# Second attention of a two-attention block: the sync queue's order written out by hand, raw weights requested and converted at set turns

## The chip, the cores and the metric

The kernel runs on one core of one Trainium2 chip. The metric is the time of one execution in microseconds (us) of device time. Before the change it is 1457.29 us, the median of three runs (1456.06 to 1458.13). The engines are TensorE (PE, matrix products), VectorE (DVE), ScalarE (ACT), GpSimd (POOL) and SyncE (SP); SP computes nothing and issues nearly all DMA transfers, in the order of its own queue.

## The reference

The input is x, 1024 tokens of 512 numbers. Four stages follow each other, each with a layernorm ahead of it and a residual sum behind it:

```python
x = x + attn_a(layernorm(x))   # 32 heads of 16, 8 groups of keys and values
x = x + ffn(layernorm(x))      # base matrix plus 2 of 8 low-rank experts per token
x = x + attn_b(layernorm(x))   # 32 query heads of 128, 8 key/value groups, 4-bit weights, causal
x = x + ffn(layernorm(x))      # the same ffn again
```

The change lies in the third, the second attention:

```python
def _dequant_matmul(x, qw, scales):
    w = (qw.astype(float32) - 8.0) * repeat(scales, 128, axis=0)
    return x @ w
q, k, v = dequant matmuls of x;  q, k = rope(q), rope(k)
scores = causal(q @ k.T / sqrt(128));  attn = softmax(scores);  ctx = attn @ v
return _dequant_matmul(ctx, qw_o, scales_o)
```

The weights qw_q, qw_k, qw_v and qw_o arrive as int32 numbers from 0 to 15.

## The kernel before, in words

The first attention, the first ffn, the second attention and the second ffn run one after another and overlap at their seams. The second attention occupies about 545 to 1390 us of the profiled execution.

**Heads and turns.** The loop over 32 query heads n (group g = n // 4, place in the group j = n % 4) has eight turns per head. Each turn takes one tile t of 128 query rows, in the order TURNS = 0, 6, 1, 7, 2, 4, 3, 5. In a turn PE makes the score product of the tile (L869); DVE adds the causal mask and finds the largest value (L877); ACT exponentiates (L881); DVE inverts the sum (L885); ACT divides (L886). One turn later `placed` has DVE transpose the tile in 32 by 32 blocks (L900), and when both tiles of a pair are done (pair 0: tiles 0 and 1, pair 1: 2 and 3, pair 2: 4 and 5, pair 3: 6 and 7) it issues four transfers on SP (L911) that put the blocks in place: 48 KB each for pair 0, 112 KB for pair 1, 176 KB for pair 2, 240 KB for pair 3. Pair 0 goes out after turn 3's score product, pair 3 after turn 4's, pair 1 after turn 7's, pair 2 after the next head's turn 0. The context products (L949) read them: `context(n, 0)` pairs 0 and 3, `context(n, 1)` pairs 1 and 2, three turns or more later.

**Two lanes of other work.** Between the turns PE is filled from two lists of generators, a `short` and a `long` one, by nominal costs and a share per turn. `short` holds the projections: in head n the queries of head n+1, in some heads the keys or values of the next group, and the output projection of the head before. A projection (`scaled`, L798 to L812) makes, for each half of the tokens, four pairs of products; ACT takes the first pair with its scale into an accumulator tile `acc` (L810), DVE adds the other three (L812). There are two `acc` tiles. For queries and keys `rotated` then needs the rotary embedding: two transfers on SP put the halves of `acc` crosswise into a tile `turned` (L822, L823; a "turned pair" below, of 128 KB each), and POOL computes `acc` times cosine (L824), `turned` times sine (L825) and their sum (L826). The output projection's fourth part goes through ACT (L987) and POOL (L988).

**Raw weights.** `whole_numbers` (L703) requests 256 KB of int32 weights on SP (L705) into a tile `r`, one buffer for each of the kinds q, k (keys and values share it) and o, and has POOL subtract 8 into a tile `w` (L706), two buffers for each kind. A new request waits until POOL has converted the tile in `r` before it; a conversion waits until PE is done with the `w` of two before it.

**Who sets the order.** Everything in the second attention is written under `manual_schedule(engines={PE})`: PE's queue keeps the order of the source. The other four queues are ordered by the scheduler of the language's tile layer, by its own estimate of when things are ready, so a request can stand in SP's queue well ahead of its place in the source or behind it. In the program that results, SP's queue before the change has, in a typical head, pair 0, the request for qwo, pair 3, turned pairs, a request for k or v, pair 1, pair 2, a turned pair, the request for q.

Of the kernel before, what the change touches and what calls it, by code (L numbers as in the profile page):

```python
# [12 lines left out]
F32R = mybir.dt.float32r  # L13
BF16 = mybir.dt.bfloat16
I32 = mybir.dt.int32
# [5 lines left out]
P = 128  # L21
S = 1024
C = 512
NC_ = C // P
NT = S // P
# [4 lines left out]
G = 8  # L30
# [11 lines left out]
def kernel(  # L42
# [630 lines left out]
    def attention_b():  # L673
# [5 lines left out]
        with ExitStack() as ph:  # L679
# [17 lines left out]
            def bank():  # L697
                return ac_ps.tile([P, C], F32, tag="acc", name="bank")

            def whole_numbers(kind, rows, n, bufs=2):  # L700

                r = work.tile([P, n], I32, tag=f"r{kind}", name="r", bufs=1)
                w = work.tile([P, n], F32R, tag=f"w{kind}", name="w", bufs=bufs)  # L703
                dst = r if len(rows.shape) == 2 else r.rearrange("p (c o) -> p c o", o=rows.shape[2])
                nc.sync.dma_start(dst, rows)  # L705
                nc.gpsimd.tensor_scalar_add(w, r, -ZERO)  # L706
                return w

            def input_weights(kind, qw, n):
                rows = qw[:, ts(n, DB)].rearrange("(c p) o -> p c o", p=P)  # L710
                return whole_numbers(kind, rows, NC_ * DB).rearrange("p (c o) -> p c o", o=DB)

            wks = {0: input_weights("k", qwk, 0)}
            wqs = {0: input_weights("q", qwq, 0)}
            wvs = {0: input_weights("k", qwv, 0)}
            wos = {0: whole_numbers("o", qwo[0:P, :], C)}
            nc.sync.dma_start(cos_sb, cos_t)

            nc.sync.dma_start(sin_sb[0:64], sin_t[64:128])
# [74 lines left out]
            def left(lane):  # L794
                return sum(item[1] for item in lane)
# [65 lines left out]
            def probabilities(n, t):  # L861

                qT, kT = qTs[n], kTs[n // J]
                keys = (t + 1) * P
                wide = t >= NT // 2 or (n == 0 and t == 1)
                sc = sc_ps.tile([P, S if wide else C], F32, tag=f"sc{wide}", name="sc")
                for k0 in range(0, keys, C):
                    k1 = min(k0 + C, keys)
                    nc.tensor.matmul(sc[:, k0:k1], qT[:, ts(t, P)], kT[:, k0:k1], start=True, stop=True)  # L869
# [12 lines left out]
                return p, total  # L882
# [7 lines left out]
            def placed(n, t, p):  # L890

                pair, first = t // 2, t // 2 * 2 + 1
                if t % 2 == 0 and pair > 1:
                    blocks[pair] = late[0].tile(
                        [P, J, (2 * first + 1) * 32], F32, tag=f"blocks{pair}", name="blocks", bufs=1
                    )
                at = t % 2 * first * 32
                nc.vector.transpose(  # L900
                    blocks[pair][:, :, at : at + (t + 1) * 32].rearrange("p j (k c) -> p k j c", c=32),
                    p.rearrange("p (k j c) -> p k j c", j=4, c=32),
                )
                if t % 2:
                    which = int(pair in SETS[1])
                    while any(m == n - 1 and int(u // 2 in SETS[1]) == which for m, u in lagging):
                        behind()
                    complete(("c", n - 1, which))
                    width = (2 * first + 1) * 32
                    for i in range(4):  # L910
                        nc.sync.dma_start(  # L911
                            place[pair][:, i],
                            blocks[pair][ts(i, 32), :, :width],
                        )
# [88 lines left out]
            with tc.manual_schedule(engines={mybir.EngineType.PE}):  # L1003
# [83 lines left out]
                    nc.vector.tensor_copy(flat[:, part.start : part.start + 1], total)  # L1087
                    nc.sync.dma_start(room[:, part], w_kept[:, part])

                def request(n):  # L1090

                    g, j = n // J, n % J
                    if j == 0 and 0 < g < G - 1:
                        wks[g + 1] = input_weights("k", qwk, g + 1)
                    if j == 2 and g + 1 < G:
                        wvs[g + 1] = input_weights("k", qwv, g + 1)

                for n in range(HEADS):
                    g, j = n // J, n % J
                    if j == 0 and 0 < g < G - 1:  # L1100
                        short.append([("k", g + 1), 16 * FAST, keys(g + 1)])
                    if j == 2 and g + 1 < G:
                        short.append([("v", g + 1), 16 * FAST, values(g + 1)])
                    if n + 1 < HEADS:
                        wqs[n + 1] = input_weights("q", qwq, n + 1)
                        short.insert(0, [("q", n + 1), 16 * FAST, queries(n + 1)])
                    shares = [
                        (left(lane) + LAST_LATER[i]) // NT
                        if n == HEADS - 1
                        else (left(lane) + LATER[i] - KEPT[i] - HELD[i] * (j % 2 == 0)) // NT  # L1110
                        if n
                        else left(lane) // 5
                        for i, lane in enumerate((short, long))
                    ]
                    for i, t in enumerate(TURNS if n else [0, 1, 2, 4, 3, 5, 6, 7]):
                        if n and i == 2:
                            wos[n] = whole_numbers("o", qwo[ts(n, P), :], C)
                        if i == 4:
                            request(n + 1)

                        p, total = probabilities(n, t)
                        lagging.append((n, t))
                        if fresh:
                            placed(*fresh.pop())
                        fresh.append((n, t, p))
                        if n == t == 0:
                            complete(("k", 0))
                            complete(("q", 0))
                            wks[1] = input_weights("k", qwk, 1)
                            short.append([("k", 1), 16 * FAST, keys(1)])  # L1130
                            shares[0] = left(short) // NT
                        fill(short, shares[0])
                        divided(p, total)
                        if n == HEADS - 1 and i:
                            reload(i - 1, total)
                        join()
                        if len(lagging) > LAG and lagging[0][0] < HEADS - 1:
                            behind()
                        fill(long, shares[1])
                    complete(("q", n + 1))  # L1140
                    if j == J - 1:
                        complete(("k", g + 1))


                xns = {
# [139 lines left out]
```

## Time and profile before

| | |
|---|---|
| median of three runs | 1457.29 us |
| profiled execution, first to last instruction (span) | 1454.8 us |
| what lies around the span, by the median | 2.5 us |
| mean granted TensorE clock | 0.994 |
| stretch 640 to 745 us (four heads): PE, DVE, ACT, POOL busy | 102.38, 93.88, 68.74, 64.15 us of 105 |
| one head in the middle of the loop | 24.9 to 27.8 us |

The profile is of one execution. A group line names the source line, the engine, what is written and read, the count, the busy time and the mean duration, and then the engine's idle time ahead of these instructions with what ended it. `SPq` is the SP queue: a line of its waits gives who waited for whom, total time, times, longest. In a timeline row the first number is the start, the second the duration (both us), and brackets hold idle time just before and what ended it; rows with x4 merge four instructions. PE's busy time is modelled and counts weight loading beside it separately (PEld).

### The profile page before, as it was taken

Reading aid. Unit: us, or ns where it says so; the run is one execution under the profiler, and the core shown is the slowest. Engines: PE = TensorE matmul, PEld = TensorE weight load, DVE = VectorE, ACT = ScalarE, POOL = GpSimd, SP = SyncE. Lnnn points to the kernel's source line nnn. Section 1 sums busy time; section 2 is a strip of 40 time slices with the busy share of each in tenths; the row PEclk is TensorE's granted clock in tenths of the full one; section 3 lists DMA queues with packets and bytes.
Section 4 is the critical chain, followed back from the end, with each engine's and each line's share of the span. In section 5 each row is a group of like instructions: output and inputs, shape, how many; then the busy total and the mean of one; then the engine's idle time right before and its main releaser. Section 6 shows DMA issues by size and latency. Waiting matters only on the chain.

```text
span 1454.8 us, 21185 instructions
## 1 busy us (share of the span) xinstructions
PE 1390.1 (96%) x6711; PEld 882.1 (61%) x6711; DVE 1190.2 (82%) x2491; ACT 868.6 (60%) x1642; POOL 539.7 (37%) x425
## 2 busy tenths in 40 slices
PE   6999999999999998999999999999999999999888
PEld 4444444444444545677777777776776777777664
DVE  4799979879892668798998988898898898989774
ACT  2176657657677226676676666666665676666630
POOL 4200000000000516556646646656566566544230
PEclk9999999999999999999999999999999999999999
DMA  4352423324240324655555655655556555555611
GB/s 126 59 103 46 72 36 62 54 39 73 40 133 2 99 73 110 144 142 149 131 143 143 145 134 135 150 141 135 148 133 150 140 137 134 136 136 120 182 65 58
DMA packets 136736, 158.48 MB, mean 109 GB/s; under 512 B 35008, under 2 KB 111488, under 8 KB 136496
## 3 DMA queue, kind: packets, MB, share of 16 engines
q1 hardware_dynamic: 136204, 156.49, 45.1%
q8 instruction: 54, 0.88, 0.3%
q0 software_dynamic: 352, 0.59, 0.2%
q14 instruction: 58, 0.48, 0.1%
q10 hardware_dynamic: 68, 0.03, 0.0%
HBM read 33.03 MB, written 6.05 MB: 27 GB/s over the span
## 4 chain that ended last, share of the span: by engine, by line
PE 70%; DVE 10%; DMA 9%; SPq 4%; POOL 3%; issue 2%; ACT 2%; ACTq 0%; POOLq 0%; DVEq 0%
PE pc L949 13%; PE sc L869 12%; PE po L408 7%; PE sc L334 7%; DVE m L343 6%; DMA xT<-blocks 6%; PE pp L799 4%; PE pp L798 4%; PE bank L607 4%; PE py L798 3%; SPq L911 3%; PE py L799 3%; DMA turned<-acc 3%; PE st L375 2%; PE py L448 2%
## 5 line engine op out<-in xcount | busy, mean ns | idle before, releaser
L387 ACT ACTIVATE pT<-st 128x512 f32<-128x512 f32 x512 | 264.6, 603 | 128.7 <-PE st L383 107.1
L343 DVE TENSOR_REDUCE m<-sc 128x1 f32<-128x512 f32 x512 | 319.8, 681 | 25.8 <-PE st L375 20.4
L869 PE MATMUL sc<-kT,qT 128*128 128x512 f32 (+3 forms) x768 | 291.6, 489 | 4.3 <-POOL qT L826 2.1
L881 ACT ACTIVATE x_sb<-x_sb,m 128x768 f32<-128x768 f32 (+7 forms) x256 | 196.9, 769 | 119.5 <-DVE m L877 116.8
L949 PE MATMUL pc<-xT,v_sb 128*128 128x256 f32 (+1 forms) x1024 | 242.0, 361 | 22.9 <-DMA xT<-blocks 22.0
L886 ACT ACTIVATE x_sb<-x_sb,total 128x768 f32<-128x768 f32 (+7 forms) x256 | 195.5, 772 | 70.7 <-DVE total L885 69.2
L949 PEld LDWEIGHTS pc<-xT,v_sb 128*128 128x128 f32 x1024 | 191.3, 190 | 59.5 <-issue 26.4
L877 DVE CUSTOM_DVE_ANT_0 x_sb<-sc,causal 128x768 f32<-128x768 f32 (+7 forms) x256 | 191.5, 748 | 36.4 <-PE sc L869 35.1
L334 PE MATMUL sc<-ks,qs 64*128 64x512 f32 x512 | 186.9, 448 | 5.3 <-DVE m L343 2.6
L798 PE MATMUL pp<-x_hl,w 128*128 128x512 f32 x384 | 183.9, 479 | 2.0 <-ACT acc L810 1.4
L869 PEld LDWEIGHTS sc<-kT,qT 128*128 128x128 f32 x768 | 138.3, 191 | 76.1 <-issue 61.2
L383 PE MATMUL st<-ms_q,ones 64*128 64x512 f32 x512 | 177.9, 413 | 0.7 <-DMA ms_q<-mT 0.7
L375 PE MATMUL st<-qs,ks 64*128 64x512 f32 x512 | 176.0, 423 | 1.4
L334 PEld LDWEIGHTS sc<-ks,qs 64*128 64x128 f32 x512 | 83.8, 184 | 146.1 <-DVE m L343 129.5
L799 PE MATMUL pp<-x_hl,w 128*128 128x512 f32 x384 | 153.4, 399 | 2.3 <-DVE x_hl L756 2.3
L900 DVE STREAM_TRANSPOSE blocks<-x_sb 128x640 f32<-128x640 f32 (+3 forms) x128 | 133.2, 1041 | 25.0 <-ACT x_sb L886 21.2
L812 DVE SCALAR_TENSOR_TENSOR acc<-pp,q_sc,acc 128x512 f32<-128x512 f32 x192 | 140.8, 733 | 14.1 <-ACT acc L810 10.3
L706 POOL TENSOR_SCALAR w<-r 128x512 fp32r<-128x512 int32 x80 | 119.6, 1495 | 80.3 <-PE pp L799 49.4
L824 POOL TENSOR_TENSOR qT<-acc,cos_sb 128x512 f32<-128x512 f32 x62 | 79.9, 1288 | 168.6 <-DVE acc L812 133.2
L127 POOL DMA_DIRECT2D shared<-in_b_base_dram x1 | 0.6, 563 | 367.3 <-DVE m L343 367.3
L408 PE MATMUL po<-pT,v_sb 128*32 128x512 f32 x1024 | 136.6, 604 | 0.0
L798 PE MATMUL py<-ctx,w 128*128 128x512 f32 x256 | 132.9, 519 | 2.1 <-ACT acc L810 1.4
(174 smaller groups left out, 2138.3 us busy)
## 6 DMA issues: line engine op xcount, KB each, us to landing
xT<-blocks SPq DMA_DIRECT2D x128, 240.0 KB, 4.4
xT<-blocks SPq DMA_DIRECT2D x128, 176.0 KB, 3.2
turned<-acc SPq DMA_DIRECT2D x160, 128.0 KB, 2.6
pT<-x_sb SPq DMA_DIRECT2D x128, 112.0 KB, 2.7
qs<-q_hl SPq DMA_DIRECT2D x128, 64.0 KB, 2.5
qs<-shared SPq DMA_DIRECT2D x128, 64.0 KB, 2.5
r<-in_qwq_dram SPq DMA_DIRECT2D x32, 256.0 KB, 2.8
r<-in_qwo_dram SPq DMA_DIRECT2D x32, 256.0 KB, 2.7
```

The lines of the kernel that those rows point to most:

```text
L334: nc.tensor.matmul(sc, qs[pair % NS][rows, jj, ts(t, P)], ks[pair // 2 % NS][rows, ts(half, C)], start=True, stop=True,)
L343: nc.vector.tensor_reduce(ms[pair][:, at : at + 1], sc, AX.X, ALU.max, negate=True)
L375: nc.tensor.matmul(st, ks[pair // 2 % NS][rows, ts(kt, P)], qs[pair % NS][rows, u // 2, ts(u % 2, C)], start=True, stop=False,)
L387: nc.scalar.activation(pTs[pair, kt][:, u], st, AF.Exp, scale=DA**-0.5)
L408: nc.tensor.matmul(po[ts(u, 32), :], v_sb[:, kt, pair // 2, :], pT[:, u], start=(kt == 0), stop=(kt == NT - 1),)
L798: nc.tensor.matmul(ps, lhsT, high, start=True, stop=False)
L799: nc.tensor.matmul(ps, lhsT, low, start=False, stop=True)
L869: nc.tensor.matmul(sc[:, k0:k1], qT[:, ts(t, P)], kT[:, k0:k1], start=True, stop=True)
L877: nc.vector.tensor_tensor_reduce(p, sc[:, :keys], causal[:, S - keys :], -1.0, BIG, ALU.add, ALU.min, m)
L881: nc.scalar.activation(p, p, AF.Exp, bias=m, scale=-1.0, accum_out=total)
L886: nc.scalar.activation(p, p, AF.Copy, scale=total)
L949: nc.tensor.matmul(pc[:, 2 * P * i + lo : 2 * P * (i + 1)], v_sb[:, k, ts(g, DB)], some, start=(k == 0), stop=(k == 2 * pair + 1),)
```

## The change

In the second attention alone, three things:

- `whole_numbers` is split into `request`, which issues the transfer into `r`, and `whole_numbers`, which converts it into `w`.
- The requests and conversions stand at set turns of a head. `ask(n, i)`, after the score product of turn i: at turn 1 the raw queries' weights of head n+2 (before, those of head n+1 at the head's start), at turn 2 those of a key or value projection that head n+1 begins, at turn 3 the output weights of head n. `convert(n, i)`, ahead of the score product: at turns 5, 6 and 7 the same three.
- The loop over the heads stands under a second `manual_schedule` for SP, so that SP's queue too keeps the order of the source within it. POOL, DVE and ACT are still ordered by the scheduler.

```diff
-            def whole_numbers(kind, rows, n, bufs=2):
-
-                r = work.tile([P, n], I32, tag=f"r{kind}", name="r", bufs=1)
-                w = work.tile([P, n], F32R, tag=f"w{kind}", name="w", bufs=bufs)
-                dst = r if len(rows.shape) == 2 else r.rearrange("p (c o) -> p c o", o=rows.shape[2])
-                nc.sync.dma_start(dst, rows)
+            raw = {}
+
+            def request(kind, name, n):
+
+                r = work.tile([P, NC_ * DB], I32, tag=f"r{kind}", name="r", bufs=1)
+                raw[name, n] = kind, r
+                if kind == "o":
+                    nc.sync.dma_start(r, qwo[ts(n, P), :])
+                else:
+                    rows = {"q": qwq, "k": qwk, "v": qwv}[name][:, ts(n, DB)]
+                    nc.sync.dma_start(
+                        r.rearrange("p (c o) -> p c o", o=DB), rows.rearrange("(c p) o -> p c o", p=P)
+                    )
+
+            def whole_numbers(name, n):
+
+                kind, r = raw.pop((name, n))
+                w = work.tile([P, NC_ * DB], F32R, tag=f"w{kind}", name="w", bufs=2)
                 nc.gpsimd.tensor_scalar_add(w, r, -ZERO)
...
-                def request(n):
+                def side_weights(n):
 
                     g, j = n // J, n % J
                     if j == 0 and 0 < g < G - 1:
-                        wks[g + 1] = input_weights("k", qwk, g + 1)
+                        return "k", "k", g + 1
                     if j == 2 and g + 1 < G:
...
+                        return "k", "v", g + 1
+
+                def ask(n, i):
+
+                    if i == 1 and n + 2 < HEADS:
+                        request("q", "q", n + 2)
+                    if i == 2 and side_weights(n + 1):
+                        request(*side_weights(n + 1))
+                    if i == 3 and n:
+                        request("o", "o", n)
+
+                def convert(n, i):
+
+                    if i == 5 and n + 2 < HEADS:
+                        whole_numbers("q", n + 2)
+                    if i == 6 and side_weights(n + 1):
+                        whole_numbers(*side_weights(n + 1)[1:])
+                    if i == 7 and n:
+                        whole_numbers("o", n)
+
+                request("q", "q", 1)
+                whole_numbers("q", 1)
+                with tc.manual_schedule(engines={mybir.EngineType.SP}):
+                    for n in range(HEADS):
...
+                        for i, t in enumerate(TURNS if n else [0, 1, 2, 4, 3, 5, 6, 7]):
+                            convert(n, i)
+                            p, total = probabilities(n, t)
+                            lagging.append((n, t))
+                            if fresh:
+                                placed(*fresh.pop())
+                            fresh.append((n, t, p))
+                            ask(n, i)
```

More of the change, by code (lines that the diff above doesn't have):

```diff
@@ L698, in bank @@
                 return ac_ps.tile([P, C], F32, tag="acc", name="bank")
-            def whole_numbers(kind, rows, n, bufs=2):
-                r = work.tile([P, n], I32, tag=f"r{kind}", name="r", bufs=1)
-                w = work.tile([P, n], F32R, tag=f"w{kind}", name="w", bufs=bufs)
-                dst = r if len(rows.shape) == 2 else r.rearrange("p (c o) -> p c o", o=rows.shape[2])
[L705 to L716, printed above, removed]
+            raw = {}
[12 more added lines that the diff above has]
+                w = work.tile([P, NC_ * DB], F32R, tag=f"w{kind}", name="w", bufs=2)
+                nc.gpsimd.tensor_scalar_add(w, r, -ZERO)
+                weights_of[name][n] = w if name == "o" else w.rearrange("p (c o) -> p c o", o=DB)
+            wks, wqs, wvs, wos = {}, {}, {}, {}
+            weights_of = {"k": wks, "q": wqs, "v": wvs, "o": wos}
+            for kind, name in (("k", "k"), ("q", "q"), ("k", "v"), ("o", "o")):
+                request(kind, name, 0)
+                whole_numbers(name, 0)
             nc.sync.dma_start(cos_sb, cos_t)
@@ L1088, in reload @@
                     nc.sync.dma_start(room[:, part], w_kept[:, part])
-                def request(n):
+                def side_weights(n):
                     g, j = n // J, n % J
                     if j == 0 and 0 < g < G - 1:
-                        wks[g + 1] = input_weights("k", qwk, g + 1)
+                        return "k", "k", g + 1
                     if j == 2 and g + 1 < G:
[L1096 to L1142, printed above, removed]
@@ new lines, in attention_b @@
+                request("q", "q", 1)
+                whole_numbers("q", 1)
+                with tc.manual_schedule(engines={mybir.EngineType.SP}):
+                    for n in range(HEADS):
+                        g, j = n // J, n % J
+                        if j == 0 and 0 < g < G - 1:
+                            short.append([("k", g + 1), 16 * FAST, keys(g + 1)])
+                        if j == 2 and g + 1 < G:
+                            short.append([("v", g + 1), 16 * FAST, values(g + 1)])
+                        if n + 1 < HEADS:
+                            short.insert(0, [("q", n + 1), 16 * FAST, queries(n + 1)])
+                        shares = [
+                            (left(lane) + LAST_LATER[i]) // NT
+                            if n == HEADS - 1
+                            else (left(lane) + LATER[i] - KEPT[i] - HELD[i] * (j % 2 == 0)) // NT
+                            if n
+                            else left(lane) // 5
+                            for i, lane in enumerate((short, long))
+                        ]
+                        for i, t in enumerate(TURNS if n else [0, 1, 2, 4, 3, 5, 6, 7]):
[6 more added lines that the diff above has]
+                            ask(n, i)
+                            if n == t == 0:
+                                complete(("k", 0))
+                                complete(("q", 0))
+                                request("k", "k", 1)
+                                whole_numbers("k", 1)
+                                short.append([("k", 1), 16 * FAST, keys(1)])
+                                shares[0] = left(short) // NT
+                            fill(short, shares[0])
+                            divided(p, total)
+                            if n == HEADS - 1 and i:
+                                reload(i - 1, total)
+                            join()
+                            if len(lagging) > LAG and lagging[0][0] < HEADS - 1:
+                                behind()
+                            fill(long, shares[1])
+                        complete(("q", n + 1))
+                        if j == J - 1:
+                            complete(("k", g + 1))
```

## The prediction

> **What bounds the kernel now.** I read the page first: the share of each engine, and the chain that ended last.
>
> ```profile
> PE 1390.1 (96%) x6711; PEld 882.1 (61%) x6711; DVE 1190.2 (82%) x2491; ACT 868.6 (60%) x1642; POOL 539.7 (37%) x425
> PE 70%; DVE 10%; DMA 9%; SPq 4%; POOL 3%; issue 2%; ACT 2%; ACTq 0%; POOLq 0%; DVEq 0%
> ```
>
> TensorE (PE) is the bound at 96%, so the change can only win what PE idles in the second attention (about 545 to 1390 us), and the chain hints at DMA and the sync queue (SP) for part of it. So I took the waits next, of SP and of PE.
>
> ```profile
> SPq L705 <- POOL w L706: 147.9, 73, 11.1
> ```
> ```profile
> PE pc L949 <- DMA xT<-blocks: 22.0, 20, 3.0
> ```
>
> The first is what the change is aimed at: 73 times SP stands in front of a raw-weight request (L705) until GpSimd (POOL) has converted the tile before it. It is large, but SP's standing still costs only where something due is queued behind. The second line is the price on PE: the context matmuls wait 20 times for transposed probabilities, 22.0 us in all. That is nearly the whole prize.
>
> All these waits are on one thing, pair 3 (tiles 6 and 7 of a head: four transfers of 240 KB). The timelines of SP, POOL, DVE and PE around one head (6) show how it comes about.
>
> ```profile
> 719.75 2.53 SPq L911 DMA_DIRECT2D xT<-xT  x4
> 725.01 0.35 SPq L705 DMA_DIRECT2D r<-in_qwo_dram  x1
> 725.47 3.94 SPq L911 DMA_DIRECT2D xT<-blocks  x4
> ```
> ```profile
> 722.27 1.25 DVE L900 STREAM_TRANSPOSE blocks<-x_sb 128x1024 f32<-128x1024 f32 x1
> ```
> ```profile
> 723.49 1.49 POOL L706 TENSOR_SCALAR w<-r 128x512 fp32r<-128x512 int32 x1
> ```
> ```profile
> 732.32 1.10 PE L949 MATMUL pc<-xT,v_sb 128*128 128x256 f32 x4 [0.81 <-DMA xT<-blocks]
> ```
>
> The transpose of tile 7 is done at 723.5. SP is waiting for the conversion (to 724.98), requests weights, and issues pair 3 at 725.47: 1.9 us late. PE uses it at 732.32, 6.85 after the first issue, having idled 0.81.
>
> I read this off for every head. A group is four heads (j = 0 to 3); heads 4 to 27 repeat it six times. "Late" is first issue of pair 3 minus end of its transposes; "deadline" is PE's use less its idle, from the same point.
> - j=0: late 1.0, deadline 8.15; PE idle 0.46, 0.85, 0.07, 0.44, 1.91, 0.37 = 4.1.
> - j=1: late 0.8 (1.6 in head 5), deadline 7.1; 1.36, 0.62, 0.75, 0.58, 0.71, 0.66 = 4.7.
> - j=2: late 1.7 to 2.0 (3.1 in head 10), deadline 8.0; 0.81, 2.54, 1.02, 0.49, 0.79, 0.84 = 6.5.
> - j=3: late 0.1, deadline 10.3; no idle.
> - Outside: head 1 0.99; heads 28 to 31 1.63, 0.20, 1.74, 3.04, with 28 to 30 issued on time (0.1), so that no order of SP can help them.
>
> From first issue to use PE took 6.8 to 7.1 us where it waited, 7.3 to 8.05 (once 9.0) in j=0 heads.
>
> **The change part by part.** The instruction lists of both programs say that PE, DVE and ACT execute the same rows in the same order; only SP and POOL are reordered, with the same 1145 transfers and 388 arithmetic instructions. So no work is added: all is a matter of what stands ahead of what.
>
> *Removed: requests that wait for POOL, conversions that wait for PE.* A raw tile is now asked for a whole head after its buffer was read, and converted into a buffer that PE left a head ago. The 147.9 us on SP go; so does POOL's own wait for PE before L706 (49.4 and 24.8 us). Worth what it does to pair 3:
>
> *j=0 and j=2.* The new list has pair 0 (4 x 0.65 = 2.6), raw qwo (0.4), one turned pair (1.25), pair 3. That is 4.25 after pair 0 is ready; pair 3's transposes end 3.8 after it. Late is then 0.5. With 6.8 to 7.6 to use, that makes 7.3 to 8.1, inside 8.15 and 8.0. I leave 1.0 in each class for strays such as head 20 (9.0). Gain 3.1 + 5.5 = 8.6. Bounds: 0, if landing slows as much as issue quickens; 10.6, all of it.
>
> *j=1.* This class has two turned pairs ahead of pair 3 already, and gets qwo's request on top.
>
> ```profile
> 693.54 2.54 SPq L911 DMA_DIRECT2D xT<-xT  x4
> ...
> 699.55 3.83 SPq L911 DMA_DIRECT2D xT<-blocks  x4
> ```
>
> Late goes from 0.8 to 1.15, straight onto PE: 0.35 x 5, less 0.4 won in head 5: a loss of 1.4 (bounds 0 and 5 x (0.35 + 0.4) = 3.8, if the 256 KB also slow the landing by 0.4, half the spread of the j=0 heads).
>
> *j=3.* Late 0.5 against 2 to 3 us of room: nothing.
>
> *The request for two heads ahead* moves in front of the first turned pair of each head (before, it stood behind it). In j=1 heads that pair is due at once: ACT's next L810 needs the accumulator that the turned transfer reads. SP's timeline and ACT's, head 5, then ACT and PE in head 17:
>
> ```profile
> 686.52 0.51 SPq L822 DMA_DIRECT2D turned<-acc  x1
> 687.07 0.61 SPq L823 DMA_DIRECT2D turned<-acc  x1
> 689.89 0.37 SPq L705 DMA_DIRECT2D r<-in_qwq_dram  x1
> ```
> ```profile
> 689.82 0.69 ACT L810 ACTIVATE acc<-pp,q_sc 128x512 f32<-128x512 f32 x1
> ```
> ```profile
> 1005.41 0.69 ACT L810 ACTIVATE acc<-pp,q_sc 128x512 f32<-128x512 f32 x1 [1.17 <-DMA turned<-acc]
> ```
> ```profile
> 1006.15 0.50 PE L798 MATMUL py<-ctx,w 128*128 128x512 f32 x1 [1.06 <-ACT acc L810]
> ```
>
> In head 5 the pair lands just in time; in head 17 it is 1.17 late and PE pays 1.06. Behind ACT's wait are the exponentials of the same turn, so pair 3 moves along and the loss adds. Price of 256 KB ahead: at least 0; at most 1.4, since pair 3's 983 KB take 5.3 us from first packet to last. Head 13 is the nearest row, by the packets' times: there pair 2's last packet ended 2.39 after the turned issue instead of head 5's 1.80, and the turned pair's 3.14 after it instead of 2.77, so 0.6 us more traffic ahead moved the landing by 0.4. The requests stand 0.5 to 1 us ahead of the pair and the late end of pair 2's transfers is there already; I take 0.5 net for each of six heads: 3.0 lost (bounds 0 and 8.4).
>
> The Trainium skill ("DMA: Bandwidth & Descriptors", section "Queues, rings and completion order") says that on each DMA engine descriptors are consumed in ring order, so a request ahead on the same queue is served first. Taken strictly that is the full 1.4 us, and the sum would be 5.4 worse; the 0.4 for 0.6 of head 13 is gentler, and the trace decides.
>
> *Head 28.* Its second turned pair (for head 29's queries) went out at 1294.99, ahead of pair 3; in the new list it stands behind it. Head 30 shows what that costs:
>
> ```profile
> 1347.76 0.56 SPq L822 DMA_DIRECT2D turned<-acc  x1
> ```
> ```profile
> 1352.32 1.27 POOL L825 TENSOR_TENSOR turned<-turned,sin_sb 128x512 f32<-128x512 f32 x1 [1.32 <-DMA turned<-acc]
> ```
> ```profile
> 1356.12 1.13 PE L869 MATMUL sc<-kT,qT 128*128 128x512 f32 x2 [1.18 <-POOL qT L826]
> ```
>
> 4.5 us from issue to L825, and PE idles 1.18. In head 28 the pair would go at 1300.4: L825 at 1304.9, done after L826 at 1307.5, where PE wanted it at 1304.4. I take 2.7 lost (bounds 1.2, head 30's row, and 4.4, with a 1.3 us L988 between).
>
> *Start (heads 0 to 2).* The second turned pair of head 0 went out 1.05 us after its data (555.87 for 554.82), behind a raw request; PE then idled 2.00 for qT. Now it goes first: 1.0 won. Head 2's pair loses a request ahead of it (0.65): 0.8 of a 0.96 idle. Head 1 gets qwo ahead of pair 3 and two requests ahead of a tight turned pair: 0.5 lost (0 to 1.5). End: qwo's request ahead of head 31's pair 3, 0.3 lost (0 to 1).
>
> *Cover.* The later second turned pair (by 4.5 us in most heads) is hidden: qT was ready 5 to 9 us before its first score matmul, and is still 3.4 to 5 ahead. Converted weights are ready 9 us or more ahead. If that cover is gone, PE waits at L869 for POOL at a head's start.
>
> **Sum.** Won: 8.6 + 1.0 + 0.8 = 10.4. Lost: 1.4 + 3.0 + 2.7 + 0.5 + 0.3 = 7.9. The span of 1454.8 becomes 1452.3; the median of the runs (1457.29) lies 2.5 above the profiled span, so 1454.8. That is 0.17% faster, and about 0.2% (2.9 us) is what a measurement of this kernel can tell from no change.
>
> **The rivals.**
> - *Only the gain.* The requests are spread by turns, and their transfers fall into DMA time that nobody needs. For it: heads 21 and 25, where pair 2's last packet ended 1.2 to 1.4 us after the turned issue, have the pair landed at 2.6, with time to spare. Against: in j=1 heads the queue is at its fullest there. Then 10.4 is won and only 1.4 (j=1's pair 3) and 1.2 (head 28's lower bound) are lost: 1457.3 - 7.8 = 1449.5; with all of 10.6 and of head 2's idle won and j=1's loss at its bound of 0, 1445.9.
> - *Slower by the tight turned pair.* The place is ACT's L810 in j=1 heads; the price the full 1.4 us in six heads (8.4) plus 1.5 in head 1; with 3.8 at j=1's pair 3, 2.7 in head 28 and 0.3 at the end that is 16.7 lost against 10.4: 1463.6. It decides from the point where the first turned pair lands over 2.8 us after its issue; head 13 (3.14) and 17 (3.97) were beyond it. Against: in four of the six such heads of the trace the pair landed in time (2.57 to 2.77), so that part of the 1.4 is absorbed.
> - *No change by substitution.* SP's wait at the raw requests turns into equal waits at turned transfers, and pair 3 stays as late as it was: 1457.
>
> **How the numbers follow.** Forecast (small mixed gain, 1451 to 1458.5) 0.42, of which 0.17 beyond 0.2% and 0.25 within; only the gain 0.20, all faster; slower 0.30, of which 0.28 beyond the bound; no change by substitution 0.08. Faster 0.37, same 0.35, slower 0.28. Range 1446 to 1463: it leaves out the far half of either rival; the likeliest case's own range is 1451 to 1458.5.
>
> **What would show it.** Right: L705's successor no longer waits for POOL in SP's waits; pair 3 goes out 0.5 after its transposes in j=0, 2 and 3, and 1.1 to 1.2 in j=1; the PE waits on xT<-blocks fall from 22 to about 14 us, in j=1 heads and at the end; ACT L810 waits for turned<-acc rise from 5.3 to some 8 us; a new PE wait on qT of 2 to 3 us near 1300. Wrong: pair 3 late by over 1 us in j=0 or 2 heads, PE waiting for POOL's qT in every head, or no wait of ACT for turned transfers.

## The result, and the profile after

The changed kernel takes **1459.99 us** (median of 20 runs, 1457.33 to 1462.26), the kernel before 1457.09 us (20 runs, 1450.47 to 1460.04). The ratio is 1.0024, with a 95% interval of 1.0014 to 1.0033: slower by 0.24%, 3.5 us, where a gain of 2.5 us was forecast. The profiled execution's span is 1458.7 us against 1454.8: 3.9 more. It has the same work on each engine, as the page of the changed kernel says:

```profile
PE 1390.4 (95%) x6711; PEld 883.8 (61%) x6711; DVE 1189.9 (82%) x2491; ACT 868.5 (60%) x1642; POOL 539.8 (37%) x425
```

Of the 3.9 us, 3.6 are idle time of PE, all of it in the second attention (ahead of it and behind it PE idles as long as before); 0.3 are busy time. (That page's chain of waits breaks off after 3% of the span and is of no use.) New line numbers: requests L707 (o) and L710 (q, k, v), conversion L718; L798 is now L807, L810 L819, L812 L821, L822/L823 L831/L832, L826 L835, L869 L878, L877 (DVE's mask and maximum) L886, L900 L909, L911 L920, L949 L958, L988 L997. In e9 to e12 below, L909, L920 and L958 are one higher.

The waits of SP. The first fence has two lines of the kernel before, the second the same two of the changed one:

```profile
SPq L911 <- DVE x_sb L900: 44.7, 20, 3.5
...
SPq L911 <- DVE xT L900: 41.4, 31, 4.3
```
```profile
SPq L920 <- DVE xT L909: 122.1, 30, 6.4
SPq L920 <- DVE x_sb L909: 93.7, 30, 4.5
```

The 147.9 us in front of requests are gone, as the change means them to be, and 130 us of them are back under another name: SP now stands in front of the tiles that DVE transposes. A wait of a queue that is not the bound does not tell by its size what taking it away is worth: here 148 us in front of requests went, and the kernel became slower.

The waits of PE, one line of the kernel before that the prediction did not show, then three of the changed kernel:

```profile
PE pc L949 <- issue: 0.8, 2, 0.6
```
```profile
PE pc L958 <- DMA xT<-blocks: 17.8, 15, 3.1
...
PE py L807 <- ACT acc L819: 6.2, 6, 1.3
PE pc L958 <- issue: 5.8, 5, 2.7
```

The line for xT<-blocks fell from 22.0 to 17.8 as if 4 us were won. But five of the waits are now put down to "issue", though pair 3's data had not landed there either: together it is 22.8 before and 23.6 after. Both lines of a consumer must be added before a gain is read from one of them.

Read off by class of head, as in the prediction, PE idles ahead of pair 3:

| | j=0 | j=1 | j=2 | j=3 | heads 28 to 31 | PE ahead of py, for ACT's L819 |
|---|---|---|---|---|---|---|
| before | 4.1 | 4.7 | 6.5 | 0 | 6.6 | 1.4 |
| after | 3.8 | 8.9 | 1.2 | 0 | 7.6 | 6.2 |

The j=2 heads gained what they should. The j=1 heads lost 9.0 us, in two places: 4.8 at L819 and 4.2 at pair 3. SP in head 5 (j=1) of the changed kernel:

```profile
681.73 2.72 SPq L920 DMA_DIRECT2D xT<-blocks  x4
684.50 0.59 SPq L710 DMA_DIRECT2D r<-in_qwq_dram  x1
685.39 0.53 SPq L831 DMA_DIRECT2D turned<-acc  x1
685.97 0.59 SPq L832 DMA_DIRECT2D turned<-acc  x1
686.61 0.60 SPq L710 DMA_DIRECT2D r<-in_qwv_dram  x1
693.43 2.53 SPq L920 DMA_DIRECT2D xT<-xT  x4
696.00 0.59 SPq L707 DMA_DIRECT2D r<-in_qwo_dram  x1
...
699.99 3.80 SPq L920 DMA_DIRECT2D xT<-blocks  x4
```

Then ACT, PE and DVE there (in brackets the idle time before the row, and what ended it):

```profile
689.74 0.69 ACT L819 ACTIVATE acc<-pp,q_sc 128x512 f32<-128x512 f32 x1 [1.08 <-DMA turned<-acc]
```
```profile
690.48 0.50 PE L807 MATMUL py<-ctx,w 128*128 128x512 f32 x1 [0.97 <-ACT acc L819]
```
```profile
690.46 0.75 DVE L821 SCALAR_TENSOR_TENSOR acc<-pp,q_sc,acc 128x512 f32<-128x512 f32 x1 [0.95 <-ACT acc L819]
...
692.93 0.43 DVE L909 STREAM_TRANSPOSE xT<-x_sb 128x256 f32<-128x256 f32 x1
...
696.60 1.25 DVE L909 STREAM_TRANSPOSE blocks<-x_sb 128x1024 f32<-128x1024 f32 x1
```

q's request stands ahead of the turned pair; the pair lands late, ACT waits 1.08, PE 0.97, DVE 0.95. DVE's transpose of 128x256, which completes pair 0, stands behind that L821, a score's L886 and another L821, at 692.93. Pair 0 therefore goes out at 693.43, then o's request and two turned pairs, and only then pair 3, 2.1 us after its transposes (697.85). Head 5 is the worst of the six; in the other five j=1 heads pair 3 is late by 1.4.

### The profile page after: what moved, and what is told of

It is laid out like the page before. It is cut to its first block, busy times and chain, and to the rows that moved or that the text cites. A ratio compares the mean times of both kernels' runs of the same rounds, so it can differ in the third digit from the quotient of the medians.

```text
span 1458.7 us, 21145 instructions
## 1 busy us (share of the span) xinstructions
PE 1390.4 (95%) x6711; PEld 883.8 (61%) x6711; DVE 1189.9 (82%) x2491; ACT 868.5 (60%) x1642; POOL 539.8 (37%) x425
## 5 line engine op out<-in xcount | busy, mean ns | idle before, releaser
L878 PE MATMUL sc<-kT,qT 128*128 128x512 f32 (+3 forms) x768 | 291.1, 488 | 3.1 <-POOL qT L835 1.3
L958 PE MATMUL pc<-xT,v_sb 128*128 128x256 f32 (+1 forms) x1024 | 244.0, 364 | 23.8 <-DMA xT<-blocks 17.8
L958 PEld LDWEIGHTS pc<-xT,v_sb 128*128 128x128 f32 x1024 | 192.6, 191 | 60.5 <-issue 25.8
L886 DVE CUSTOM_DVE_ANT_0 x_sb<-sc,causal 128x768 f32<-128x768 f32 (+7 forms) x256 | 191.4, 748 | 34.1 <-PE sc L878 33.0
L807 PE MATMUL pp<-x_hl,w 128*128 128x512 f32 x384 | 183.0, 476 | 1.2 <-DVE acc L821 0.9
L878 PEld LDWEIGHTS sc<-kT,qT 128*128 128x128 f32 x768 | 138.5, 191 | 74.7 <-issue 60.9
L718 POOL TENSOR_SCALAR w<-r 128x512 fp32r<-128x512 int32 x80 | 119.2, 1490 | 118.8 <-DMA r<-in_qwq_dram 91.3
L909 DVE STREAM_TRANSPOSE blocks<-x_sb 128x640 f32<-128x640 f32 (+3 forms) x128 | 133.2, 1041 | 27.4 <-ACT x_sb L895 20.5
L821 DVE SCALAR_TENSOR_TENSOR acc<-pp,q_sc,acc 128x512 f32<-128x512 f32 x192 | 140.8, 733 | 16.3 <-ACT acc L819 12.2
L807 PE MATMUL py<-ctx,w 128*128 128x512 f32 x256 | 132.7, 518 | 6.9 <-ACT acc L819 6.2
```

What stands on the lines that cost most here:

```text
L807: nc.tensor.matmul(ps, lhsT, high, start=True, stop=False)
L886: nc.vector.tensor_tensor_reduce(p, sc[:, :keys], causal[:, S - keys :], -1.0, BIG, ALU.add, ALU.min, m)
L958: nc.tensor.matmul(pc[:, 2 * P * i + lo : 2 * P * (i + 1)], v_sb[:, k, ts(g, DB)], some, start=(k == 0), stop=(k == 2 * pair + 1),)
```

## The experiments

Each run lists its granted clock (0.987 to 0.998 for the kernels of the table). Over all their runs a line fits with 1.04 us less time for 0.001 more clock; the column "at 0.994" sets each kernel's mean to one clock by it (standard errors 0.1 to 0.9 us). Ratios are to the kernel before and are not so adjusted. The six columns on the right are PE's idle time in the profiled execution, in us: ahead of pair 3 by class of head; ahead of py (the output projection) for ACT's L810 or L819; and ahead of the scores sc, for qT for the most part. "Late" is used as in the prediction.

POOL's queue is still ordered by the scheduler in all of these programs, so its list changes with every edit but that from e5 to e9 (by 5 to 52 of its 425 rows between the kernels compared below, 114 in e6). PE's list is the same in all of them. DVE's and ACT's are too, save where the text says otherwise and for one row of ACT in e1 and e3.

| run | median | ratio, 95% | at 0.994 | j=0 | j=1 | j=2 | 28-31 | py | sc |
|---|---|---|---|---|---|---|---|---|---|
| before | | | 1456.0 | 4.1 | 4.7 | 6.5 | 6.6 | 1.4 | 4.3 |
| after | 1459.99 | 1.0024, 1.0014-1.0033 | 1459.5 | 3.8 | 8.9 | 1.2 | 7.6 | 6.2 | 3.1 |
| e1 q behind | 1456.04 | 0.9998, 0.9984-1.0011 | 1454.9 | 3.9 | 8.8 | 0.8 | 6.6 | 0.1 | 3.0 |
| e2 o behind | 1458.65 | 1.0021, 1.0008-1.0034 | 1457.1 | 1.6 | 6.5 | 0.4 | 6.3 | 6.0 | 6.8 |
| e3 both | 1455.05 | 0.9987, 0.9971-1.0002 | 1452.9 | 1.3 | 7.3 | 0.0 | 5.8 | 1.0 | 7.3 |
| e4 small request | 1472.38 | 1.0101, 1.0078-1.0125 | 1469.3 | 3.4 | 10.2 | 2.3 | 8.2 | 7.1 | 8.0 |
| e5 o at turn 6 | 1448.50 | 0.9940, 0.9923-0.9957 | 1447.4 | 1.0 | 6.8 | 0.4 | 6.1 | 1.9 | 3.1 |
| e7 two ahead | 1456.18 | 1.0001, 0.9990-1.0012 | 1455.2 | 3.2 | 0.6 | 2.2 | 7.6 | 10.9 | 2.8 |
| e8 third acc | 1462.38 | 1.0038, 1.0025-1.0050 | 1456.9 | 6.5 | 9.5 | 2.3 | 7.5 | 0.0 | 5.7 |
| e9 transpose first | 1443.58 | 0.9908, 0.9889-0.9927 | 1443.4 | 1.0 | 2.5 | 0.2 | 6.7 | 1.7 | 3.1 |
| e10 transpose alone | 1452.03 | 0.9970, 0.9956-0.9984 | 1450.3 | 3.6 | 2.1 | 0.9 | 6.9 | 5.4 | 2.7 |
| e11 before + transpose | 1453.77 | 0.9982, 0.9971-0.9993 | 1451.9 | 4.0 | 0.8 | 6.9 | 6.0 | 1.7 | 4.4 |
| e12 o past pair 1 | 1440.99 | 0.9896, 0.9877-0.9915 | 1441.3 | 1.4 | 0.7 | 0.1 | 6.1 | 1.9 | 3.0 |

**e1, q's request behind the turned pair.**

```
-                    if i == 1 and n + 2 < HEADS:
+                    if i == 2 and n + 2 < HEADS:
                         request("q", "q", n + 2)
```

> One edit to the changed kernel: q's raw request goes out one turn later, behind the head's first turned pair instead of ahead of it; the rest as changed. Theory (what stands ahead on SP's queue is what lands late): the turned pair of the j=1 heads lands before ACT wants it, the six PE waits on ACT's L819 there (6.2 us) fall to about 1.4 as in the kernel before; the span falls by 3 to 5 us, to about 1454 to 1456. Rival (the new traffic itself, wherever it stands, slows the transfers): the waits stay at 5 us or more and the span within 1 us of the changed kernel's 1458.7. Both: pair 3 of the j=1 heads stays as late as it is (1.4), its waits at 8 to 10 us.

Measured: 4.6 us less than the changed kernel at the same clock, and py waits 0.1 for L819 in place of 6.2. In the j=1 heads the turned pair's last packet ends 2.55 to 2.85 us after its issue, as in four of the six heads before (2.57 to 2.77); in the changed kernel it was 3.44 to 3.85. So the theory held, and the rival (traffic, wherever it stands) did not. Pair 3 stayed as late, as both expected.

**e2, o's request behind pair 3.**

```
-                    if i == 3 and n:
+                    if i == 4 and n:
                         request("o", "o", n)
```

> One edit to the changed kernel: o's raw request goes out one turn later, behind pair 3 instead of ahead of it. Theory (order on SP's queue): pair 3 goes out 0.6 us sooner in all heads (late 1.4 to 0.8 in j=1, 0.7 to 0.1 in j=0 and 2); PE's waits on pair 3 fall from 8.9 to about 5 us in the j=1 heads and from 3.8 to about 2 in the j=0 heads; the span falls by 5 to 6 us, to about 1453. ACT's L819 waits stay (6 us of PE). Rival (what pair 3 gains in issue its transfer loses, as in the j=0 heads, where it was 0.3 us less late and PE waited as long): less than 2 us won.

Measured: late falls by 0.6 in the j=1 heads (to 0.8) and to 0.2 in most j=0 and j=2 heads; pair 3's waits fall by 6.3 us in all. But the time falls by 2.3 only, not 5 to 6: in heads 1, 28 and 30 the second turned pair stands behind pair 3, and o's request is now in front of it. PE pays for it at the starts of heads 2 (1.7) and 31 (3.2):

```profile
PE sc L878 <- POOL qT L835: 4.9, 2, 3.2
```

In the changed kernel that line is 1.3, 1, 1.3. The request went from the front of one due transfer to the front of another.

**e3, both.** Both edits above.

> Both edits together. Theory: the gains add, 8 to 11 us below the changed kernel's span, about 1449; PE's waits on pair 3 in the j=1 heads 4 to 5 us, ACT's L819 waits 1.4 us, pair 3 of the j=2 heads still without a wait. Rival (traffic, not order): within 2 us of the changed kernel. A second rival: with q later, POOL converts it later, and its rope operations and so qT come late at a head's start: then a wait on qT of over 0.5 us a head appears.

Measured: the gains add (4.6 and 2.3 make 6.9; 6.6 found), less than the 8 to 11 expected, for the same qT waits (sc 7.3) and since pair 3 in j=1 heads still costs 7.3, more than in the kernel before (4.7) with the same late of 0.8.

**e4, a small request in o's old place.**

```
+                    if i == 3 and n:
+                        nc.sync.dma_start(work.tile([P, 4], I32, tag="none", name="none", bufs=1), qwo[ts(n, P), :4])
```

> As the one with o's request behind pair 3, and in its old place ahead of pair 3 a request of 2 KB (128 x 4 numbers, never read): it costs SP an issue and moves almost no bytes. It tells issue time from bytes. If SP's issue slot is the cost, pair 3 is as late as in the changed kernel (1.3 to 1.4 in j=1) and PE waits 8 to 9 us there. If the 256 KB ahead on the rings are the cost, pair 3 is late by the slot, yet lands sooner, and PE's waits are nearer to those of the kernel with o behind (5 us) than to the changed kernel's.

Measured: 12.2 us above e2, which differs by these 31 requests and by the place of six POOL rows: 0.39 us for each request. The operations of the tile "none", with least, median and longest ns:

```profile
L1116 SPq DMA_DIRECT2D none<-in_qwo_dram x31: 341/590/1147, 591.4 to 1379.7; - x31
```

2 KB take SP as long as 256 KB (0.59). Pair 3 is late by 1.4 in all j=1 heads, as with the whole request there, and PE waits even longer. So at pair 3 of the j=1 heads the price of a request ahead is SP's issue: its bytes add little or nothing. In the changed kernel, with 256 KB ahead, pair 3's last packet came 6.44 to 6.96 us after its issue there (6.63 on average; 6.55 in the kernel before, with no request ahead); in e4, with 2 KB ahead, it came at 6.82 to 6.99. It is not sooner in e4 although the bytes ahead are gone; but the 256 KB now stand behind pair 3, which costs 0.3 by e12 below. The Trainium skill ("DMA: Bandwidth & Descriptors", section "Issuing engines are not separate DMA queues") says that the time to initiate a DMA is usually small relative to the DMA itself. Here it was 0.59 us for a request of 2 KB, and at pair 3 it cost more than the bytes of a whole request did.

**e6, the fixed order alone.** The kernel before, its head loop put under the fixed order of SP, nothing else:

```
+                with tc.manual_schedule(engines={mybir.EngineType.SP}):
                     for n in range(HEADS):
```

> One part of the change alone: the kernel before, with its requests and conversions together as they were (one head ahead), and only the sync queue held to the source's order. The other part alone needs no run: without the fixed order the scheduler makes of the changed source the very instruction lists of the kernel before, on all five engines. Theory: requests that stand behind a conversion in a fixed order make SP wait for POOL, and in the source q's request stands at a head's first turn and o's ahead of pair 0; SP's wait on POOL stays above 100 us in all, pair 3 is late where such a wait falls ahead of it, but q's request is not close ahead of the first turned pair in the j=1 heads, so that ACT's L810 waits stay small (under 2 us). Time 1455 to 1462. Rival (a fixed order of SP by itself brings the loss): ACT's waits for turned transfers rise to 6 us as in the changed kernel.

Measured: 1719.5 us (4 runs), ratio 1.1798 (1.1777 to 1.1818). Both expectations fell: the loss is neither at pair 3 nor at ACT. PE's waits, and PE and POOL at the start of a head:

```profile
PE pp L798 <- POOL w L706: 200.7, 30, 8.7
```
```profile
614.63 1.49 POOL L706 TENSOR_SCALAR w<-r 128x512 fp32r<-128x512 int32 x1 [2.47 <-DMA r<-in_qwq_dram]
```
```profile
616.17 0.80 PE L798 MATMUL pp<-x_hl,w 128*128 128x512 f32 x1 [8.69 <-POOL w L706]
```

In the source of before, a head requests q's weights and multiplies by them in the same head; it was the scheduler that moved the request forward, to three heads ahead of that (the ninth request, for head 8, goes out at 664.4, in head 4). Held to the source's order, PE waits for request, landing and conversion once a head. These stops are 5.4 to 8.7 us long. PE was granted 0.88 to 0.89 of its clock in this stage (the kernel before: 0.99 over the same stage), and its busy time for the same instructions rose from 1390.1 to 1463.4 us; so the kernel lost more than the length of the stops. DVE's and ACT's lists changed too (186 and 90 rows). The changed source without the fixed order gives the kernel before's instruction lists on all engines. So the new places in the source act only through the fixed order of SP, and asking earlier is what the fixed order needs, not a gain of its own. Whether it has to be two heads earlier is not tested.

**e7, the suspected cost doubled.**

```
-                    if i == 2 and side_weights(n + 1):
+                    if i == 1 and side_weights(n + 1):
```

> The changed kernel with the suspected cost doubled: the side request (v's in the j=1 heads, k's in some j=3 heads) stands with q's ahead of the first turned pair. Theory: the second request costs the pair about another issue slot and some of its transfer, 0.6 to 1.2 us in each of six heads, all of it on ACT and PE since the pair is already beyond its due time: PE's waits on ACT's L819 rise from 6.2 to between 10 and 14 us, and the time by 4 to 7 us over the changed kernel. In the j=3 heads nothing, the pair is not due there. Rival (the wait is POOL's or DVE's doing, not the pair's): no more than 1 us.

Measured: PE's waits on L819 rose to 10.9, as expected:

```profile
PE py L807 <- ACT acc L819: 10.9, 6, 2.6
```

and yet the kernel was 4.3 us *faster* than the changed one. Pair 3's waits in the j=1 heads had gone from 8.9 to 0.6. The instruction lists show an edit that was not meant: in these six heads the scheduler had also moved DVE's transpose of tile 1 ahead of L821. By itself, therefore, e7 could not price the second request. It led to e9 and e10.

**e8, a third accumulator buffer.**

```
-                    acc = work.tile([P, C], F32, tag="acc", name="acc")
+                    acc = work.tile([P, C], F32, tag="acc", name="acc", bufs=3)
...
-                        part = work.tile([P, C], F32, tag="part", name="part", bufs=2)
+                        part = work.tile([P, C], F32, tag="part", name="part", bufs=1)
```

> The changed kernel's order of SP untouched, the request still ahead of the tight turned pair, but what makes ACT wait for it is gone: a third accumulator buffer (and, for room, one buffer of part instead of two). Theory: the turned pair lands as late as before and nobody waits; PE's waits on ACT's L819 fall from 6.2 to under 1 us, and the time falls by 3 to 5 us at the same clock, as with q's request behind the pair. Pair 3 stays as late. Rival (the pair's lateness hurts elsewhere, in POOL's rope and qT): the time stays within 1.5 us. The single part buffer may cost ACT a wait for POOL at L996 of up to 1 us a head.

Measured: no PE wait on L819 is left, so it was the accumulator that held ACT. But the time is not the 3 to 5 us less: 2.6 at the same clock, with a ratio of 1.0038 as measured (its runs had the lowest clock, 0.989). The scheduler reordered DVE and ACT too (80 and 51 of their rows stand elsewhere), and pair 3 lost another 5.6 us. It confirms the mechanism and tells nothing of the size.

**e9, e10, e11: tile 1's transpose first.** The same edit on three kernels: on e5 (o's request at turn 6, converted in the next head), on the changed kernel, and on the kernel before.

```
-                nc.vector.transpose(
...
+                with tc.high_priority() if t == 1 and n % J == 1 and n > 1 else ExitStack():
+                    nc.vector.transpose(
...
```

> The changed kernel with that one move on DVE alone; SP's order is the changed kernel's. Theory: the loss at pair 3 of the j=1 heads (8.9 us of PE's waits, late 1.4) came of o's request and two turned pairs standing between a late pair 0 and pair 3; with pair 0 sooner SP clears them in time, pair 3 is late by 0.1 and its waits there fall to 0.6 as in the run with two requests ahead, in which the scheduler had made the same move; ACT's L819 waits stay at 6 us. The time falls by 7 to 8 us to 1452 at the same clock. The run with two requests ahead, which stood 3 us above that, then shows the second request's price: 0.6 to 0.8 us in each of six heads. Rival (the second request itself helped): the waits on pair 3 stay at 8 us.

> The kernel before with that move on DVE alone. Theory: there too pair 0 is what makes pair 3 late in the j=1 heads (0.8): PE's 4.7 us of waits there fall to under 1, the time by 4 us to about 1452. The j=0 and j=2 heads keep their 4 and 6.5 us. If instead the move takes nothing away there, pair 0's lateness mattered only with o's request behind it.

Measured, e10: 9.2 us under the changed kernel. SP's, ACT's and PE's lists are the changed kernel's. On DVE the transpose moves in seven heads (29 too), and in six of them one row of the output projection changes places with an L821. DVE and SP of e10 in head 5:

```profile
690.75 0.40 DVE L910 STREAM_TRANSPOSE xT<-x_sb 128x256 f32<-128x256 f32 x1
...
692.22 0.75 DVE L821 SCALAR_TENSOR_TENSOR acc<-pp,q_sc,acc 128x512 f32<-128x512 f32 x1 [0.50 <-ACT acc L819]
...
698.33 1.25 DVE L910 STREAM_TRANSPOSE blocks<-x_sb 128x1024 f32<-128x1024 f32 x1 [0.39 <-ACT x_sb L895]
```
```profile
691.21 2.53 SPq L921 DMA_DIRECT2D xT<-xT  x4
693.79 0.59 SPq L707 DMA_DIRECT2D r<-in_qwo_dram  x1
...
699.64 3.88 SPq L921 DMA_DIRECT2D xT<-blocks  x4
```

Pair 0 goes out 8.4 us ahead of pair 3 instead of 6.6; SP has got through o's request and both turned pairs in time, and pair 3 leaves 0.1 us after its transposes (699.58). Its waits in the j=1 heads are 2.1, of which 1.7 in one head, against 8.9; that is 6.8 of the 9.2. e11 (SP's list differs from that of the kernel before in two rows): 4.2 us at the same clock (0.18% as measured), j=1's waits 4.7 to 0.8. So there too DVE's order made pair 3 late. e7 less e10 then prices the second request ahead of the turned pair: 4.9 us in time, 5.5 in PE's waits on L819 (10.9 and 5.4), some 0.8 to 0.9 in each of six heads, about what the first cost (4.8). The two programs also differ in k's request in j=3 heads, in how far the transpose moved and in 24 POOL rows, so this price is less clean than the first.

**e5, e9, e12: the version that came out of it.** e5 is e1 with

```
-                    if i == 3 and n:
+                    if i == 6 and 0 < n < HEADS - 1 or i == 4 and n == HEADS - 1:
                         request("o", "o", n)
...
-                    if i == 7 and n:
-                        whole_numbers("o", n)
+                    if i == 1 and n > 1:
+                        whole_numbers("o", n - 1)
+                    if i == 7 and n == HEADS - 1:
+                        whole_numbers("o", n)
```

> The version with both requests behind, with o's request two turns later still: at turn 6, after pair 3 has landed and after the second turned pair, converted at turn 1 of the next head (head 31's at its own turn 4 and 7). Theory: with no raw bytes among pair 3's packets its last packet ends 6.5 us after its issue instead of 6.8 to 7.0, PE's waits on pair 3 fall from 7.3 to about 4.5 us in the j=1 heads; the qT waits at the starts of heads 2 and 31 (1.9 and 3.3 us), which o's request ahead of the second turned pair brought, go. Together 4 to 7 us below that version at the same clock: 1448 to 1451, clearly faster than the kernel before. Rival: the bytes now fall among pair 1's and pair 2's packets and delay those, or POOL's later conversion delays qT: within 1 us of that version.

> The version with o's request at turn 6 and q's behind the turned pair, plus one move on DVE: in the j=1 heads the transpose of tile 1 (128x256, 0.42 us), which completes pair 0, goes ahead of the rope's L821, which waits for ACT's L819. Theory: in the j=1 heads pair 0's four issues are then through before pair 3 is ready; pair 3 goes out on time (late 0.1 to 0.3 instead of 0.8), PE's waits on it there fall from 6.8 us to under 1.5, and the time by about 5 us, to 1442 to 1444, 0.9% under the kernel before. Rival (pair 3's deadline comes sooner by as much, or the two turned pairs hold it up all the same): less than 2 us.

e12 is e9 with one turn more:

```
-                    if i == 6 and 0 < n < HEADS - 1 or i == 4 and n == HEADS - 1:
+                    if i == 7 and 0 < n < HEADS - 1 or i == 4 and n == HEADS - 1:
```

> The version with tile 1's transpose first and both requests behind, with o's request one turn later still, behind pair 1. At turn 6 it had in SP's list the same place as at turn 4, right behind pair 3, since SP has nothing between, and it ran ahead: 150 to 190 KB of other packets still lay among pair 3's, whose last packet ended 6.85 after its issue in the j=1 heads. Theory (bytes right behind a transfer share its rings and delay its end): with them gone the last packet ends at 6.45 to 6.55 as in the kernel before, PE's waits on pair 3 fall from 2.5 to about 1 us in the j=1 heads and by about 1 us in heads 28 to 31, and the time by 1 to 4 us, to 1440 to 1442. Rival: o now lies ahead of pair 2 and so of the tight first turned pair of the j=1 heads; ACT's L819 waits rise from 1.7 to 4 us or more and the time is the same or up to 3 us longer.

Measured: e5 won 5.5 on e3, but not as expected. Its qT waits did go (sc 7.3 to 3.1); pair 3's last packet did not come sooner (6.7 to 7.4 us after its issue in the j=1 heads). SP's list shows why: nothing stands between turns 4 and 7, so a request of turn 6 follows right behind pair 3 all the same: the lists of e3 and e5 differ in the place of three requests on SP (heads 1, 28 and 30) and of five rows on POOL. e9 then won 4.0 (5 expected; j=1's waits 6.8 to 2.5, not under 1.5), and e12 2.1 more (standard error 0.8): its pair 3 ends 6.49 to 6.57 after its issue in the j=1 heads, where e9's ends at 6.80 to 6.89. So 150 to 190 KB of packets right *behind* pair 3 cost it 0.3 us. The rival of e12 did not come: its waits of PE are

```profile
PE pc L959 <- DMA xT<-blocks: 9.8, 8, 2.5
PE py L807 <- ACT acc L819: 1.8, 2, 1.5
```

e12 beats both kernels: 1440.99 us, ratio 0.9896 (0.9877 to 0.9915), 1% under the kernel before.

## Why the prediction was wrong

The step that failed is the price of the requests that the change puts ahead of due transfers. 2.5 us were to be won, and PE idled 3.65 more, a swing of 6.2. At pair 3 the j=1 heads account for 2.8 of it and the j=0 heads for another 2.8: there o's request was priced at 0.35 to 0.4 us of SP's time, and pair 3 in the j=0 heads was taken to land sooner after its issue than it does. At the first turned pair of the j=1 heads 1.8 came on top. The other terms together were 1.2 better than forecast. Taken step by step, in the profiled executions:

- **j=2, 5.5 to be won**: 5.3. Right in size, and in mechanism: pair 3 goes out sooner and meets its deadline. But late was 0.75 in four heads and 1.3 to 1.6 in two, not 0.5; in the four the room made it harmless, the two waited 0.7 and 0.4. (The 6.8 to 7.1 us from issue to use were 7.4 and 7.2 in heads 10 and 14.)
- **j=0, 3.1 to be won**: 0.3. The step took 0.5 for late; it came to 0.7 in four heads and 1.3 to 1.4 in two. It took 6.8 to 7.6 us from issue to use, though the prediction's own reading of these heads was 7.3 to 8.05; it came to 7.6 to 8.2. Pair 3's last packet, 6.8 to 7.15 us after its issue in five of six heads before, came at 7.2 to 7.7 in five. The lower bound, "landing slows as much as issue quickens", is nearly what happened. With o's request out of the way (e2) late is 0.2 in four heads and the waits are 1.6, so o's request accounts for 2.2 of the 2.8. Why the packets come so late in this class, and later still after the change, is not shown.
- **j=1, pair 3, 1.4 to be lost**: 4.2, beyond the bound of 3.8. The price of o's request was read from the row at 725.01, 0.35 us, an issue of an SP that had stood waiting. In a train of issues the same request takes 0.54 to 0.60 and 0.1 to the next, and late went to 1.4 in five heads, not 1.15, and in head 5 from 1.6 to 2.1, where 0.4 was to be won. The deadline stayed at 7.1, as assumed, so that all of it fell on PE: 3.5 us, and 0.6 more for a later landing in two heads. What the step did not see is why pair 3 was late there at all: pair 0 comes late from DVE, behind L821 (e10, e11).
- **j=1, the first turned pair, 3.0 to be lost**: 4.8 (0.8 in each of six heads). Mechanism, place and the limit were right: the pair decided from 2.8 us after its issue, and landed at 3.44 to 3.85. The size was taken from head 13's 0.4 us; measured are 0.9 at the landing and 0.8 at PE, and about as much for a second request (e7 less e10). By the Trainium skill's rule of ring order ("DMA: Bandwidth & Descriptors", section "Queues, rings and completion order"), taken strictly, a request ahead costs its full 1.4 us, an estimate from this trace's rate. The measured 0.9 lies in the middle between that and the 0.4 that head 13 gave.
- **Head 28, 2.7 to be lost to qT**: no wait on qT; 1.05 lost at head 28's own pair 3 (1.63 to 2.68). The prediction held that no order of SP could help that pair; it could hurt it: issued on time as before, its last packet came 7.4 instead of 6.5 us after its issue, with the turned pair now right behind it (that this is the cause is not shown). qT was ready at 1307.48, as forecast (1307.5). The wrong part was the need: 1304.4 is the score of tile 0, which reads qT's first half, and the late half is first read by tile 6, at 1306.85 in the kernel before and, shifted, at 1309.04 now. That no wait came is in part luck: without the shift it would have been short by 0.6.
- **Start, 1.3 net to be won; end, 0.3 to be lost**: 0.8 won up to head 3, where head 0's own pair 3 lost 1.3 that no term had; 0.1 lost at head 31's pair 3, and nothing over heads 29 to 31 together.

Won 0.3 + 5.3 + 0.8 = 6.4 of 10.4; lost 4.2 + 4.8 + 1.05 = 10.05 against 7.9: 3.65 in all, PE's added idle time.

Of the signs named beforehand, ACT's waits for turned transfers rose from 5.3 to 7.9, as forecast. But PE's waits for pair 3 did not fall to 14, no wait on qT came near 1300, and a sign of being wrong came true: pair 3 was late by over 1 us in heads 4, 12 (j=0), 18 and 26 (j=2).

The rival "slower by the tight turned pair" has the mechanism that decided, at 0.8 instead of 1.4 a head; it needed the second step, pair 3 of the same heads, to outweigh the gain. "Only the gain" and "no change by substitution" are out as wholes, though the latter is what happened in the j=0 heads and, at transposed tiles in place of turned transfers, in SP's waits.

Not settled: why head 13 of e10 waited 1.7 with pair 3 issued on time; and which part of e5's gain over e3 beyond the 4.2 us of sc is real (5.5 with a standard error of 0.9).

## What to carry to other kernels

When a queue's order is fixed by hand, price every request by its issue in a train of issues (0.6 us here, for 2 KB as for 256 KB), and by its bytes too where a small due transfer stands right behind it (0.9 us here). Ask for each place which due transfer that is: a request moved from the front of one to the front of another (e2) wins little. Look upstream of a late transfer as well: here 0.4 us of DVE work standing behind a blocked multiply was worth 4 us in the kernel before and 9 in the changed one, more than the whole change. And read a half-late buffer at the instruction that reads the late half.

## What the runs showed of the hardware

- SP took 0.5 to 0.6 us for most DMAs issued in a row, 2 KB or 256 KB (a raw request issued after a wait: 0.35). It took longer, 0.8 to 1.9 us, for some: in the changed kernel for half of pair 3's (240 KB each) and a fifth of pair 2's (176 KB each).
- A turned pair of 2 x 128 KB landed 0.9 us later with a 256 KB request directly ahead (the changed kernel against e1); 150 to 190 KB right behind pair 3 made its last packet 0.3 us later (e9 against e12).
- The granted clock of single runs lay between 0.987 and 0.998, and 0.001 of it went with 1.04 us of a 1456 us kernel: differences of 2 us need many runs or that correction. One profiled span is not enough: e2's was 6.1 us under the changed kernel's, and its runs, at one clock, 2.3.
- With a stop of PE of 5.4 to 8.7 us in each head the granted clock was 0.88 to 0.89 in that stage, against 0.99 before (e6; no run sets the stops apart from what else differs there).
